# Products with the values in runs of seven key blocks, halves of one PSUM bank by turns, eight buffers of turned weights

## The chip, the cores and the metric

The kernel runs on one core of a Trainium2 chip. The metric is the device time of one launch in microseconds (us), the median of three runs; lower is better.

## The reference, cut to what matters

A transformer block in float32: `x` is 8 x 1024 x 512, 16 heads of width 32, a causal attention and a feed-forward net with blockwise four-bit rounding. Both take the same normalised input, and both results are added to `x`.

```python
xn = layernorm(x)
q, k, v = split(xn @ W_attn + b_attn)              # 16 heads of 32
att = softmax(where(causal, q @ k.T / sqrt(32), -inf))
y = (att @ v).reshape(B, S, D)                     # the products of this change
attn = y @ W_proj + b_proj
ffn = fp4_linear(silu(fp4_linear(xn, w_gate)) * fp4_linear(xn, w_up), w_down)
out = x + attn + ffn                               # fp4_linear rounds both operands, in blocks of 16
```

## The kernel before, in words

A **tile** is 128 of the 1024 rows of one batch (64 tiles), a **twin** two neighbouring tiles, a **unit** two heads of one batch (64 units). A **pair** is two neighbouring query tiles of a unit, 256 queries; a unit has pairs 0 to 3. Pair p sees 2(p+1) key blocks of 128 keys because of the causal mask, so a unit has 2 + 4 + 6 + 8 = 20 blocks.

The program has one instruction stream per engine, in the order in which the Python code emits it (`manual_schedule`); semaphores between engines are added by the framework from the tiles that each instruction reads and writes. The order is made by a planner in the kernel: six streams of work (`merge`: products with the values `weigh`, scores `scored`, the network, its quantised input, the preparation of later tiles, and `finish`) are stepped by turns. Each step states its cost on TensorE, the time from which it may start, and how many banks it needs; `clock`, `act(...)`, `dve(...)` and `pool(...)` are the planner's own reckoning of time. `Later(us, action)` emits an action when the planner's clock has passed its due time; `.now()` emits it at once.

PSUM holds six banks for everyone (`Banks`), one bank for `acc` (the network's sum) and one for `y`.

`scored` (L604 on TensorE) makes scores in a bank, VectorE finds the negated maxima (L617, L620), ScalarE writes the exponentials to one of twelve `part` buffers (L576). `weigh(un, pair)` then goes over the key blocks j of the pair: four TensorE transposes (L709) put the block's weights, keys on partitions, into a bank (two on the last, diagonal block); ScalarE copies the bank to `pr` (L712; five buffers). Blocks are gathered in `waiting`. At every fourth key block, and at the last one of the pair, the step ends with the time from which `pr` is ready, and `weighted()` emits the products of the gathered blocks without a break (L687). The blocks are taken in groups of 2; 4; 4 and 2; 4 and 4 for the four pairs, six groups or **runs** a unit. A block gives two products (one per head) with 128x32 weights, each of which is two records in the profile; even and odd blocks and the two heads go to four column positions of the array:

```python
row = (j % 2 * HU + r) * HD
nc.tensor.matmul(y[row : row + HD, base + q0 : base + QW], ...,
    start=(j < 2), stop=(j >= last - 1), tile_position=(0, row))
```

Pair 0 and 2 write columns 0 to 255 of `y`, pair 1 and 3 columns 256 to 511 (`base`). After pair 1 and after pair 3 ScalarE copies the whole bank to `yu` (L733), and two DMAs store it to `y_kept` (L739). `emptied[0]` is the planned end of that copy; the next products wait for it in the plan.

Around it: `residual` (L790) loads the rows of `x` that the network's sum of a tile is added to (`res`, two buffers; bias on GpSimd, L793), for the first tile of a twin in the middle of its sum and for the second one before the last piece of the first. `summed` (L801) adds and later stores `part_kept` (L804). `added` makes the sum (L776), eleven products for a tile. `fetch` loads what `finish` needs: two `yT`, sixteen rows of inverses, and `part` (L890, two buffers); `finish` makes the projection (L918), adds it to `part` (L923) and stores the result (L931).

`project` (L449, then ScalarE L461) makes the queries and keys: eight products of 256 columns fill the two halves of a bank, then two ScalarE instructions read a half each:

```python
for j in range(2):
    for c in range(NC):
        nc.tensor.matmul(pq[:, j, :], lhsT=halves[j][:, c, :], rhs=xnT[:, c, :], ...)
...
for j in range(2):
    nc.scalar.activation(full[:, j, :], pq[:, j, :], AF.Identity, ...)
```

Of the kernel before, what the change touches and what calls it, by code (L numbers as in the profile page):

```python
# [9 lines left out]
F32 = mybir.dt.float32  # L10
# [9 lines left out]
P = 128  # L20
# [7 lines left out]
def kernel(  # L28
# [31 lines left out]
    nc = tc.nc  # L60

    B, S, D = x.shape
# [16 lines left out]
    SOONER = 0.45  # L79
    PARTS = 12  # L80
    QUEUE = 1.0
    LATE = 0.6
    SURE = 0.4
    FILL = 0.4
# [10 lines left out]
    p2 = ctx.enter_context(tc.tile_pool(name="p2", bufs=2))  # L95
    p3 = ctx.enter_context(tc.tile_pool(name="p3", bufs=3))
    p4 = ctx.enter_context(tc.tile_pool(name="p4", bufs=4))
    p5 = ctx.enter_context(tc.tile_pool(name="p5", bufs=5))
    p8 = ctx.enter_context(tc.tile_pool(name="p8", bufs=8))
    dram = ctx.enter_context(tc.tile_pool(name="dram", bufs=6, space=DRAM))  # L100
    ps_g = ctx.enter_context(tc.tile_pool(name="ps_g", bufs=1, space=PSUM))
# [33 lines left out]
    def act(columns, after=0.0, function="other"):  # L135
        if function == "other":
            function = table[0]
        switch = TABLE if function != table[0] else 0.0
        table[0] = function
        return on("act", 0.17 + 0.00083 * columns + switch, after)  # L140
# [525 lines left out]

    def weigh(un, pair):
        f, r0 = un.u * HU // HPC, un.u * HU % HPC
        Q, first, base = pair * QT // QG, pair * QT, pair * QT % QG * P
        last = first + QT - 1  # L670
        if pair == 0:
            units_begun[0] = un.n
            if un.n + 1 < N:
                Later(1.0, lambda: load_values(units[un.n + 1]))
        while un.there.get(last) is None:
            yield 0.0, clock[0] + 0.5, 0
        if base == 0:
            un.y = ps_a.tile([P, W], F32, name="y")
        y = un.y
        waiting = []  # L680

        def weighted():
            for j, pr, q0 in waiting:
                h, jj = j // QG, j % QG
                for r in range(HU):
                    row = (j % 2 * HU + r) * HD
                    nc.tensor.matmul(  # L687
                        y[row : row + HD, base + q0 : base + QW],
                        lhsT=un.vs[h][:, jj, r * HD : (r + 1) * HD],
                        rhs=pr[:, r, q0:],  # L690
                        start=(j < 2),
                        stop=(j >= last - 1),
                        skip_group_check=True,
                        tile_position=(0, row),
                    )
            return 0.2 + 0.22 * len(waiting)

        ready = 0.0
        for j in range(last + 1):
            h = j // QG  # L700
            i0 = max(0, j - first)
            yield 0.0, un.there[last], 1
            bank, turned = banks.take()
            turned = turned.rearrange("p (r t) -> p r t", r=HU)
            for r in range(HU):
                for i in range(i0, QT):
                    part, at = un.held[first + i, h, r]
                    at += j % QG * P
                    nc.tensor.transpose(turned[:, r, i * P : (i + 1) * P], parts[part][:, at : at + P], ident)  # L709
            cost = 0.11 * HU * (QT - i0)  # L710
            pr = p5.tile([P, HU, QW], F32, name="pr")
            nc.scalar.copy(pr[:, :, i0 * P :], turned[:, :, i0 * P :])  # L712
            ready = act(HU * (QW - i0 * P), clock[0] + cost)
            banks.back(bank, ready)
            q0 = i0 * P
            if j == 1 and q0 > 0:
                nc.gpsimd.memset(pr[:, :, :q0], 0.0)
                ready = max(ready, pool(0.2))
                q0 = 0
            waiting.append((j, pr, q0))  # L720
            if j == last or j % QG == QG - 1:
                for i in range(QT):
                    for part in sorted({un.held[first + i, h, r][0] for r in range(HU)}):
                        parts_free.append(part)
                yield cost, max(ready, emptied[0]), 0
                yield weighted(), 0.0, 1
                waiting = []
            else:
                yield cost, 0.0, 1
        if last % QG < QG - 1:  # L730
            return
        yu = p2.tile([P, W], F32, name="yu")
        nc.scalar.copy(yu, y)  # L733
        emptied[0] = act(W, clock[0] + 0.3)

        def store():
            rows = slice(r0 * HD, (r0 + HU) * HD)
            for part in range(2):
                nc.sync.dma_start(  # L739
                    out=un.batch.y[part, f, rows, Q * W : (Q + 1) * W],  # L740
                    in_=yu[part * HU * HD : (part + 1) * HU * HD, :],
                )
            un.batch.units_done += Q

        Later(emptied[0] - clock[0] + 0.5, store)
        yield 0.0, 0.0, 1

    emptied = [0.0]

    def network(twins):  # L750
        emptied = [0.0]

        def down(job):
            twin = job.twin
            yield from job.hq.wait()
            twin.pieces.append((job, job.hq.done().rearrange("p (j t) -> p j t", t=QW)))
            if job.first == 0:
                twin.acc = ps_a.tile([P, D], F32, name="acc")
            if job.last:
                residual(twin.tiles[1])  # L760
            yield 0.0, max(job.hq.end, emptied[0] if job.first == 0 else 0.0), 0
            yield from added(twin, 0, *twin.pieces[-1])

# [6 lines left out]
        def added(twin, i, job, hqT):  # L770
            tl = twin.tiles[i]
            for j in range(job.count):
                n = job.first + j
                if n == NI // 2 and i == 0:
                    residual(tl)
                nc.tensor.matmul(  # L776
                    twin.acc,
                    lhsT=hqT[:, j, i * P : (i + 1) * P],
                    rhs=wdT[:, n, :],
                    start=(n == 0),  # L780
                    stop=(n == NI - 1),
                )
                if n == NI - 1:
                    summed(tl, twin.acc, clock[0] + 0.86)
                if j % 2 == 1 or j == job.count - 1:
                    yield 0.86 * (j % 2 + 1), 0.0, 0

        def residual(tl):
            tl.xr = p2.tile([P, D], F32, name="res")
            nc.sync.dma_start(out=tl.xr, in_=x[tl.b, tl.t * P : (tl.t + 1) * P, :])  # L790

            def with_bias():
                nc.gpsimd.tensor_tensor(tl.xr, tl.xr, bp, ALU.add)  # L793
                pool(1.35)

            tl.biased = Later(6.0, with_bias)

        def summed(tl, acc, after):
            xr = tl.xr
            tl.biased.now()  # L800
            nc.vector.tensor_tensor(xr, acc, xr, ALU.add)  # L801
            emptied[0] = dve(0.7, after)
            tl.part = dram.tile([P, D], F32, name="part_kept", bufs=NT + 10)
            tl.stored = Later(emptied[0] - clock[0] + 1.0, lambda: nc.sync.dma_start(out=tl.part, in_=xr))  # L804

        def product(job, wT):
            while job.twin.xqT is None:
# [60 lines left out]
    def fetch(tl):  # L868

        t = tl.t  # L870
        cols = slice(t * P, (t + 1) * P)
        if tl.b == B - 1:
            both = p3.tile([P, 2, NC, P], F32, name="ks")
            parts = [both[:, part] for part in range(2)]
            more = p3.tile([P, 2, NC, P], F32, name="qs")
            inv, part = more[:, 0], more[:, 1].rearrange("p c t -> p (c t)")
        else:
            parts = [p1.tile([P, NC, P], F32, name=f"yT{part}") for part in range(2)]
            inv = p1.tile([P, NC, P], F32, name="inv_y")
            part = p2.tile([P, D], F32, name="part")  # L880
        for k, yT in enumerate(parts):
            nc.sync.dma_start(out=yT, in_=tl.batch.y[k, :, :, cols].rearrange("f p t -> p f t"))
        heads = tl.batch.inverses.rearrange("(f u) q r t -> q u r f t", u=HPC // HU)
        for r in range(HPC):
            nc.sync.dma_start(
                out=inv[r * HD : (r + 1) * HD],
                in_=heads[t // QG, r // HU, r % HU, :, t % QG * P : (t % QG + 1) * P].partition_broadcast(HD),
            )
        tl.stored.now()
        nc.sync.dma_start(out=part, in_=tl.part)  # L890
        tl.inputs = parts[0], parts[1], inv, part
        tl.fetched = clock[0] + 6.0
# [70 lines left out]
    class Unit:  # L963
        def __init__(self, n):
            self.n, self.b, self.u = n, n // NU, n % NU
            self.qs, self.ks, self.vs, self.held, self.there = [], [], [], {}, {}

        @property
        def batch(self):
# [214 lines left out]
```

## Time and profile before

| | |
|---|---|
| time, median of 3 runs | 4106.52 us (4104.47 to 4106.9) |
| the profiled execution: its own time | 4106.01 us |
| its span, first to last instruction | 4104.2 us |
| TensorE busy, share of the span | 4007.1 us, 98% |
| VectorE, ScalarE, GpSimd busy | 3074.7 (75%), 2155.6 (53%), 150.9 us (4%) |
| mean granted TensorE clock | 0.993 |

Each row of the profile's groups names line, engine, operation, output and inputs, shapes and count, then the busy time in us, the mean duration in ns, and the idle time of the engine just before, with what ended most of it. Matmuls are pipelined: one lasts longer in the profile than the distance from its start to the next one's start, and their ends are modelled. So the cost of a product is read from the distance of starts, not from its duration.

### The profile page before, as it was taken

Reading aid. Unit: us, or ns where it says so; the run is one execution under the profiler, and the core shown is the slowest. Engines: PE = TensorE matmul, PEld = TensorE weight load, DVE = VectorE, ACT = ScalarE, POOL = GpSimd, SP = SyncE. Lnnn points to the kernel's source line nnn. Section 1 sums busy time; section 2 is a strip of 40 time slices with the busy share of each in tenths; the row PEclk is TensorE's granted clock in tenths of the full one; section 3 lists DMA queues with packets and bytes.
Section 4 is the critical chain, followed back from the end, with each engine's and each line's share of the span. In section 5 each row is a group of like instructions: output and inputs, shape, how many; then the busy total and the mean of one; then the engine's idle time right before and its main releaser. Section 6 shows DMA issues by size and latency. Waiting matters only on the chain.

```text
span 4104.2 us, 66108 instructions
## 1 busy us (share of the span) xinstructions
PE 4007.1 (98%) x22868; PEld 2998.3 (73%) x22868; DVE 3074.7 (75%) x7128; ACT 2155.6 (53%) x5342; POOL 150.9 (4%) x202
## 2 busy tenths in 40 slices
PE   8889999999999999999999999999999999999997
PEld 7767777777777777777777777777777677767675
DVE  7886777767777777777777777777767878888774
ACT  2246565555555555555555555555555555555540
POOL 0000000000000000000000000000000000000000
PEclk9989999999999999999999999999999999999999
DMA  6654444454655555555554555555554433333314
GB/s 192 197 173 132 123 123 117 135 153 141 169 155 153 156 154 143 167 156 154 154 156 144 164 156 156 152 156 146 162 152 121 116 96 91 92 92 98 96 57 128
DMA packets 550894, 572.21 MB, mean 139 GB/s; under 512 B 112416, under 2 KB 415520, under 8 KB 550560
## 3 DMA queue, kind: packets, MB, share of 16 engines
q1 hardware_dynamic: 550560, 567.99, 49.7%
q8 instruction: 181, 2.97, 0.3%
q14 instruction: 153, 1.25, 0.1%
HBM read 399.51 MB, written 168.30 MB: 138 GB/s over the span
## 4 chain that ended last, share of the span: by engine, by line
PE 92%; DVE 5%; DMA 1%; ACT 1%; issue 1%; SPq 0%; DVEq 0%; ACTq 0%
PE bank L815 29%; PE acc L776 15%; PE bank L709 11%; PE bank L449 10%; PE bank L604 8%; PE y L687 8%; PE bank L918 5%; PE bank L494 5%; PE bank L329 1%; DVE bank L620 1%; DVE hid L322 0%; DVE hid L321 0%; DVE scale L301 0%; DVE hid L320 0%; DMA qs<-inv_kept 0%
## 5 line engine op out<-in xcount | busy, mean ns | idle before, releaser
L712 ACT COPY pr<-bank 128x512 f32<-128x512 f32 (+1 forms) x1280 | 657.4, 549 | 750.3 <-PE bank L709 697.9
L576 ACT ACTIVATE part<-bank,neg 128x512 f32<-128x512 f32 (+3 forms) x1536 | 881.9, 586 | 238.6 <-DVE neg L620 228.3
L604 PE MATMUL bank<-ks,qs 128*128 128x512 f32 (+3 forms) x1536 | 701.3, 482 | 10.0 <-ACT part L576 5.4
L776 PE MATMUL acc<-wdT,hid 128*128 128x512 f32 x1408 | 672.7, 598 | 11.7 <-DVE hid L264 10.0
L815 PE MATMUL bank<-xqT,wgT 128*128 128x256 f32 x2816 | 666.9, 381 | 0.0
L709 PEld LDWEIGHTS bank<-ident,part 128*128 128x128 f32 x4608 | 548.2, 141 | 157.9 <-issue 88.7
L815 PE MATMUL bank<-xqT,wuT 128*128 128x256 f32 x2816 | 660.7, 381 | 0.1
L709 PE MATMUL bank<-ident,part 128*128 128x128 f32 x4608 | 650.4, 274 | 3.6 <-ACT part L576 3.4
L815 PEld LDWEIGHTS bank<-xqT,wuT 128*128 128x128 f32 x2816 | 520.1, 190 | 78.9 <-issue 9.4
L815 PEld LDWEIGHTS bank<-xqT,wgT 128*128 128x128 f32 x2816 | 518.0, 190 | 77.9 <-issue 16.7
L617 DVE TENSOR_REDUCE neg<-bank 128x1 f32<-128x512 f32 x512 | 351.6, 687 | 173.3 <-PE bank L604 169.1
L604 PEld LDWEIGHTS bank<-ks,qs 128*128 128x128 f32 x1536 | 280.1, 190 | 212.4 <-issue 149.9
L776 PEld LDWEIGHTS acc<-wdT,hid 128*128 128x128 f32 x1408 | 250.2, 191 | 185.4 <-issue 162.7
L620 DVE CUSTOM_DVE_ANT_0 bank<-bank,mask 128x128 f32<-128x128 f32 (+3 forms) x512 | 246.7, 507 | 152.4 <-PE bank L604 135.1
L687 PE MATMUL y<-pr,vs 128*32 128x256 f32 (+1 forms) x5120 | 356.2, 372 | 4.1 <-ACT pr L712 4.1
L620 DVE CUSTOM_DVE_ANT_0 bank<-bank,mask,neg 128x128 f32<-128x128 f32 (+3 forms) x512 | 284.5, 556 | 98.3 <-PE bank L604 81.6
L449 PE MATMUL bank<-xnT,wa 128*128 128x256 f32 x1536 | 349.7, 381 | 0.8 <-ACT part L576 0.8
L449 PEld LDWEIGHTS bank<-xnT,wa 128*128 128x128 f32 x1536 | 286.3, 190 | 48.1 <-issue 11.0
L576 ACT ACTIVATION_READ_ACCUMULATOR part<-bank,neg 128x1 f32 x1536 | 318.2, 207 | 0.0
L461 ACT ACTIVATE full<-bank,bqk 128x256 f32<-128x256 f32 x256 | 107.5, 471 | 385.7 <-PE bank L449 335.6
L832 DVE TENSOR_TENSOR hid<-hid,bank 128x512 f32<-128x512 f32 x192 | 123.6, 644 | 237.6 <-PE bank L815 237.3
L687 PEld LDWEIGHTS y<-pr,vs 128*32 128x32 f32 x5120 | 128.7, 109 | 185.1 <-issue 83.7
(79 smaller groups left out, 4255.6 us busy)
## 6 DMA issues: line engine op xcount, KB each, us to landing
wa<-in_L_attn_W_attn_dram SPq DMA_DIRECT2D x146, 512.0 KB, 3.9
qs<-qk_kept SPq DMA_DIRECT2D x512, 128.0 KB, 3.9
ks<-qk_kept SPq DMA_DIRECT2D x512, 128.0 KB, 3.8
wp<-in_L_attn_W_proj_dram SPq DMA_DIRECT2D x81, 512.0 KB, 3.6
qk_kept<-high SPq DMA_DIRECT2D x128, 256.0 KB, 3.0
qk_kept<-full SPq DMA_DIRECT2D x128, 256.0 KB, 2.9
y_kept<-yu SPq DMA_DIRECT2D x256, 128.0 KB, 2.4
yT<-y_kept SPq DMA_DIRECT2D x112, 256.0 KB, 3.9
```

The lines of the kernel that those rows point to most:

```text
L449: nc.tensor.matmul(pq[:, j, :], lhsT=halves[j][:, c, :], rhs=xnT[:, c, :], start=(c == 0), stop=(c == NC - 1),)
L494: nc.tensor.matmul(pv[:, i, :], lhsT=xnT[:, c, i * P : (i + 1) * P], rhs=wa[:, c, :], start=(c == 0), stop=(c == NC - 1),)
L576: nc.scalar.activation(parts[part][:, j * n : (j + 1) * n], banks.tiles[bank][:, j * n : (j + 1) * n], AF.Exp, bias=least, scale=1.0 if h ...
L604: nc.tensor.matmul(sc[:, j * n : (j + 1) * n], lhsT=un.qs[Q][:, r, i * P : (i + 1) * P], rhs=un.ks[h][:, r, :n], start=True, stop=True,)
L617: nc.vector.tensor_reduce(neg[:, 1, k : k + 1], one, AX.X, ALU.max, negate=True)
L620: nc.vector.tensor_tensor_reduce(one, one, mask[:, W - n :], scale=-1.0, scalar=neg[:, 1, k : k + 1] if Q else 3e38, op0=ALU.add, op1=ALU.min,
L687: nc.tensor.matmul(y[row : row + HD, base + q0 : base + QW], lhsT=un.vs[h][:, jj, r * HD : (r + 1) * HD], rhs=pr[:, r, q0:], start=(j < 2) ...
L709: nc.tensor.transpose(turned[:, r, i * P : (i + 1) * P], parts[part][:, at : at + P], ident)
L712: nc.scalar.copy(pr[:, :, i0 * P :], turned[:, :, i0 * P :])
L776: nc.tensor.matmul(twin.acc, lhsT=hqT[:, j, i * P : (i + 1) * P], rhs=wdT[:, n, :], start=(n == 0), stop=(n == NI - 1),)
L815: nc.tensor.matmul(job.g[:, j * QW : (j + 1) * QW], lhsT=wT[:, c, n * P : (n + 1) * P], rhs=job.twin.xqT[:, c, :], start=(c == 0), stop=(c ...
L918: nc.tensor.matmul(po, lhsT=yT[:, c, :], rhs=wp[:, c, :], start=(c == 0), stop=(c == NC - 1))
```

## The change

`weigh` gathers blocks in `un.waiting`, across the borders of pairs, and emits products when seven blocks wait or the unit's last block is reached: runs of 7, 7 and 6 blocks, three a unit. The `y` tile is taken once for the whole kernel; pair p uses its half p % 2. As soon as the last block of a pair has been emitted, inside the run, `empty` emits ScalarE's copy of that half (128x256) to `yu`, now four copies a unit, and plans two DMAs of 64 KB each. `pr` has eight buffers. To make room, `res` and `part` have one buffer instead of two and `yu` is half as wide; the load of `res` for a twin's second tile comes 4 us after the first tile's sum, and `fetch` first emits the store of the tile before.

```diff
+    RUN = 7
-    p5 = ctx.enter_context(tc.tile_pool(name="p5", bufs=5))
...
-        if base == 0:
-            un.y = ps_a.tile([P, W], F32, name="y")
-        y = un.y
-        waiting = []
         def weighted():
-            for j, pr, q0 in waiting:
+            cost = 0.2 + 0.22 * len(un.waiting)
+            for j, pr, q0, pair in un.waiting:
                 h, jj = j // QG, j % QG
+                base, last = pair % 2 * QW, pair * QT + QT - 1
                 for r in range(HU):
                     ...
-            return 0.2 + 0.22 * len(waiting)
+                if j == last:
+                    emptied[pair % 2] = clock[0] + cost
+                    empty(pair)
+            un.waiting = []
+            return cost
+
+        def empty(pair):
+            yu = p2.tile([P, QW], F32, name="yu")
+            base = pair % 2 * QW
+            nc.scalar.copy(yu, y[:, base : base + QW])
+            emptied[pair % 2] = act(QW, emptied[pair % 2])
+
+            def store():
                ...
+                un.batch.units_done += pair == PAIRS - 1
+            Later(emptied[pair % 2] - clock[0] + 0.5, store)
...
-            pr = p5.tile([P, HU, QW], F32, name="pr")
+            pr = p8.tile([P, HU, QW], F32, name="pr")
...
-            waiting.append((j, pr, q0))
+            un.waiting.append((j, pr, q0, pair))
             if j == last or j % QG == QG - 1:
                ...
-                yield cost, max(ready, emptied[0]), 0
+            if len(un.waiting) == RUN or j == NT - 1:
+                yield cost, max(ready, emptied[pair % 2]), 0
                 yield weighted(), 0.0, 1
...
+    emptied = [0.0, 0.0]
+    y = ps_a.tile([P, W], F32, name="y")
...
-            if job.last:
-                residual(twin.tiles[1])
...
                 if n == NI - 1:
-                    summed(tl, twin.acc, clock[0] + 0.86)
+                    if i > 0:
+                        twin.second.now()
+                    summed(tl, twin.acc, clock[0] + 0.86, twin if i == 0 else None)
...
-            tl.xr = p2.tile([P, D], F32, name="res")
+            tl.xr = p1.tile([P, D], F32, name="res")
...
+            if twin is not None:
+                twin.second = Later(emptied[0] - clock[0] + 4.0, lambda: residual(twin.tiles[1]))
...
+        if tl.n > 0 and tl.b < B - 1 and tiles[tl.n - 1].written is not None:
+            tiles[tl.n - 1].written.now()
...
-            part = p2.tile([P, D], F32, name="part")
+            part = p1.tile([P, D], F32, name="part")
```

More of the change, by code (lines that the diff above doesn't have):

```diff
@@ L668, in weigh @@
         f, r0 = un.u * HU // HPC, un.u * HU % HPC
-        Q, first, base = pair * QT // QG, pair * QT, pair * QT % QG * P
+        first = pair * QT
         last = first + QT - 1
@@ L695, in weighted @@
                     )
-            return 0.2 + 0.22 * len(waiting)
+                if j == last:
[9 more added lines that the diff above has]
+            def store():
+                rows = slice(r0 * HD, (r0 + HU) * HD)
+                for part in range(2):
+                    nc.sync.dma_start(
+                        out=un.batch.y[part, f, rows, pair * QW : (pair + 1) * QW],
+                        in_=yu[part * HU * HD : (part + 1) * HU * HD, :],
+                    )
+                un.batch.units_done += pair == PAIRS - 1
+            Later(emptied[pair % 2] - clock[0] + 0.5, store)
         ready = 0.0
@@ L724, in weigh @@
                         parts_free.append(part)
-                yield cost, max(ready, emptied[0]), 0
+            if len(un.waiting) == RUN or j == NT - 1:
+                yield cost, max(ready, emptied[pair % 2]), 0
                 yield weighted(), 0.0, 1
-                waiting = []
             else:
                 yield cost, 0.0, 1
[L730 to L748, printed above, removed]
+    emptied = [0.0, 0.0]
+    y = ps_a.tile([P, W], F32, name="y")
     def network(twins):
@@ L796, in residual, with summed @@
             tl.biased = Later(6.0, with_bias)
-        def summed(tl, acc, after):
+        def summed(tl, acc, after, twin):
             xr = tl.xr
@@ L965, in __init__ @@
             self.n, self.b, self.u = n, n // NU, n % NU
-            self.qs, self.ks, self.vs, self.held, self.there = [], [], [], {}, {}
+            self.qs, self.ks, self.vs, self.waiting, self.held, self.there = [], [], [], [], {}, {}
         @property
```

## The prediction

> **What bounds the kernel now.** I read the page first, then TensorE's waits, then the tile view of `y`, the groups by form, and the timeline around single runs. From the page:
>
> ```profile
> PE 4007.1 (98%) x22868; PEld 2998.3 (73%) x22868; DVE 3074.7 (75%) x7128; ACT 2155.6 (53%) x5342; POOL 150.9 (4%) x202
> L687 PE MATMUL y<-pr,vs 128*32 128x256 f32 (+1 forms) x5120 | 356.2, 372 | 4.1 <-ACT pr L712 4.1
> ```
>
> TensorE is busy for 98%, and the two largest entries among its waits are small:
>
> ```profile
> PE bank L329 <- DVE hid L322: 20.7, 7, 4.6
> PE bank L329 <- DVE xt L383: 15.9, 1, 15.9
> ...
> PE y L687 <- ACT pr L712: 4.1, 8, 0.5
> ```
>
> So nothing else is to be won by waiting less: time is saved only by taking less of TensorE, and every new idle time of TensorE adds to the end in full. In the windows of 1000 to 2000 and 2000 to 3000 us TensorE is busy for 1000.00 of 1000.
>
> What a run costs beside its products is read from starts on the timeline of TensorE:
>
> ```profile
> 2004.36 3.62 PE L494 MATMUL bank<-wa,xnT 128*128 128x256 f32 x16
> 2007.91 0.63 PE L687 MATMUL y<-pr,vs 128*32 128x256 f32 x8
> 2008.47 1.99 PE L918 MATMUL bank<-wp,yT 128*128 128x256 f32 x8
> ...
> 2048.05 1.06 PE L687 MATMUL y<-pr,vs 128*32 128x256 f32 x16
> 2049.03 0.44 PE L604 MATMUL bank<-ks,qs 128*128 128x384 f32 x1
> ```
>
> Records of 256 columns follow each other by 0.216 us (L494: median of 961 distances). In a run four records, one per column position, start within 0.02 us, and the next four 0.216 us later (0.240 after the first four). So 8 records (two blocks) need 0.432 us and 16 need 0.864; from the run's start to the next work the trace has 0.568 and 1.003 us in the mean of 128 and 256 runs. That is 0.14 us too much at the way out. On the way in, the record before a run stands 0.309 us ahead of it where it is a 256-column one of L815 (99 runs, 0.093 us too much); after a score product of L604 (196 runs) it is 0.508 against 0.333 ahead of other work (0.175). The mean over the 384 runs is 0.13. One run less saves 0.27 us.
>
> **The change part by part.**
>
> *Half as many runs.* 6 become 3 a unit, 192 fewer: 192 x 0.27 = -52 us. Bounds: 192 x 0.14 = -26 (if the way in costs the same elsewhere) and 192 x 0.31 = -60.
>
> *Runs of odd length.* Even and odd blocks use different column positions, so a stretch takes as long as its longer side. Before, stretches of 2, 4, 4, 2, 4, 4 blocks gave 10 x 0.432 = 4.32 us a unit. Now the unit is cut at the runs and at the ends of pairs into 2 | 4 | 1, 5 | 2, 6 blocks: 0.432 + 0.864 + 0.432 + 1.08 (three odd blocks, the last of half width) + 0.432 + 1.296 = 4.54. 64 x 0.216 = +14 us.
>
> *Copies inside the run.* This is the part that decides. `empty` puts ScalarE's copy of one half of `y` between products, and the products behind it write the other half of the same bank. Whether they wait for the copy is shown by a case of the same shape, L449 and L461, where ScalarE's first instruction reads half of a bank and the second the other half:
>
> ```profile
> 2037.46 3.62 PE L449 MATMUL bank<-xnT,wa 128*128 128x256 f32 x16
> ...
> 2041.12 0.84 ACT L461 ACTIVATE full<-bank,bqk 128x256 f32<-128x256 f32 x2 [4.85 <-PE bank L449]
> ```
>
> The first half is complete after 8 of the 16 records, near 2037.46 + 7 x 0.216 + 0.38 = 2039.4, and ScalarE has been idle for 4.85 us; yet it starts at 2041.12, 0.04 after the last record of the other half. A bank is guarded as a whole. In the other direction, which counts here, the kernel before has six places where a TensorE write to columns 128 to 255 of a bank waits for exactly the ScalarE instruction that reads columns 0 to 127 of it; in the other 204 places of disjoint columns a wait that was already passed covers it. So TensorE waits at every copy that is followed by products in its run: after pair 0 and pair 1 in the first run, after pair 2 in the second. After pair 3 the run ends, and the next one is far off. 3 x 64 = 192 waits, one for each switch that is saved.
>
> The Trainium skill speaks against this part: PSUM — Partial Sum Buffer, section "PSUM bank collisions raise a hardware error", has the rule "Semaphore-guard PSUM by bank × quadrant (by bank is the simple version), not by address", since two engines on one bank and the same 32 partitions collide even at different columns. By that rule the 192 waits stand and the sum is the +126 us below; guarded by address it would be the -23 of the third case. No run here shows a collision.
>
> The price of one wait, ScalarE being free, from the tile view of `y` (durations as least, median and most; then what ScalarE waited for ahead of its copy, us and times) and the groups by form:
>
> ```profile
> L687 PE MATMUL y<-pr,vs x5120: 272/379/637, 253.1 to 3978.7; 128*32 128x256 f32 x167, 128*32 128x128 f32 x30
> ...
>   PE y L687: 155.0, 92
> ```
>
> ```profile
> L712 ACT COPY pr<-bank 128x256 f32<-128x256 f32 x256 | 96.9, 379 | 26.7 <-PE bank L709 26.7
> L733 ACT COPY yu<-y 128x512 f32<-128x512 f32 x128 | 75.1, 587 | 155.1 <-PE y L687 155.0
> ```
>
> From the start of the last product: 0.379 to its end; 0.080 from there to the copy's start (each of the 92 copies that waited for TensorE, out of 128); 0.379 for a copy of 128x256; 0.052 from a ScalarE end to TensorE's start (the 8 waits of L687 for L712); 0.024 more in the first four records; less the 0.216 that the next start would have taken anyway. That is 0.698 us, and 192 x 0.698 = +134 us. Nothing lies beside it: TensorE works in order, and behind the waiting product stand the rest of the run and all other streams.
>
> ScalarE is not always free. In this run the copy that belongs to the products at 2048.05 (over at 2049.11) starts 2.46 us late, since an exponential ahead of it waits for VectorE:
>
> ```profile
> 2050.33 0.69 ACT L576 ACTIVATE part<-bank,neg 128x512 f32<-128x512 f32 x1 [2.29 <-DVE neg L620]
> ...
> 2051.57 0.58 ACT L733 COPY yu<-y 128x512 f32<-128x512 f32 x1
> ```
>
> Before, that cost nothing, since the products that need the bank were planned later. Taking for all 384 runs what the code emits to ScalarE ahead of the run's products, and when it ended in the trace: in 126 runs it ends later than a copy could start, in the mean over all 0.43 us after a whole run and 0.53 after its first two blocks. Per unit two waits meet such a queue (the second one of the first run finds it drained). Bounds: 0, and 64 x (0.43 + 0.53) = +61. I take half, +30: TensorE is some 1.5 us later per run than the planner reckons, time in which ScalarE and VectorE catch up.
>
> *What is covered.* 256 copies of 0.379 instead of 128 of 0.587: +22 us on ScalarE, which is idle for 1949. 256 more DMA issues on SP, about 0.4 us each, 100 us of a queue that spends most of its time waiting; behind them stand the loads of keys, queries and weights, for which TensorE waited less than 5 us in all. Eight buffers of `pr` are what a run of seven needs. `res`: the load at 4 us after the first sum has behind it 3.3 us to landing and 1.3 for the bias, 8.6 in all, against the 11 x 0.86 = 9.5 us of the second sum; if that cover is gone, 32 twins x about 1 us. `part`: the store goes out ahead of some 18 issues of `fetch`, longer than the 4.9 us it takes to land. I cost all of this at nothing.
>
> *Sum*, against the profiled execution's 4106.0 us (0.5 below the median of the three): -52 + 14 + 134 + 30 = +126, **4232 us**, slower by 3.1%.
>
> **The rivals.**
>
> *ScalarE late at every first copy.* Same waits, but the queue ahead of the copy holds exponentials that wait for VectorE nearly each time: a late queue costs 0.434 x 384 / 126 = 1.32 us, and at 128 copies 169 us in place of 30: 4371. It decides from about two late copies in three. For it: runs of seven come when scores are dense. Against it: one in three is late now.
>
> *A single `res` or `part` in the way.* SP waits for a buffer, and loads behind it come late. At a whole landing of 2.4 us for each of 64 tiles, 64 x 2.4 = +154 on top: 4386. Against it: TensorE waits for DMA nowhere now.
>
> *Halves that are independent* (the faster side). If products wait only for a copy of their own half, one dependency in a run is left: pair 2's first block on pair 0's copy, with pair 1's 0.864 us between, more than the 0.62 that a free ScalarE takes, so only its late cases count, some 15 us. -52 + 14 + 15 = -23, 4083. It decides as soon as TensorE's row for L687 shows no wait for L733. Against it: the six waits on disjoint columns, and L461.
>
> **How the numbers follow.** 0.82 for the forecast, 0.09 for the late ScalarE, 0.03 for the single buffers, 0.06 for independent halves. The forecast's own bounds are -60 + 14 + 134 + 0 = +88 (4194) and -26 + 14 + 134 + 61 = +183 (4289). The range is reached a little below for the planner's new order of all streams, and up toward the late ScalarE: 4175 to 4325. About 0.2% (8 us) is what a measurement can tell from no change. Faster has the independent halves, 0.06; within 0.2% 0.01; slower 0.93.
>
> **What would show it.** Right: TensorE's waits get a new first entry, `y` L687 for `yu` L733, 100 to 200 us over up to 192 waits; 192 runs, of which 128 are broken by idle times; distances at ways in and out as before. The idle share of TensorE rises from 2% to about 5%. Wrong: no such entry (then the third case), or that entry far over 200 us (the first rival), or waits for DMA or for `res` L801 beside it (the second).

## The result and the profile after

The changed kernel takes 4270.42 us (median of 4 runs, 4265.94 to 4275.31), the kernel before 4105.5 us on the same chip (4 runs, 4102.65 to 4106.9). The ratio is 1.0398 (95% interval 1.0385 to 1.0411): slower by 4.0%, 165 us; 4232 us were forecast, with 4175 to 4325 as the range. The profiled execution took 4265.94 us with a span of 4264.2 us, 160 us longer than before. First the page of the changed kernel: busy times and shares of the span, and the group of the products with the values.

```profile
PE 4017.3 (94%) x22868; PEld 3042.2 (71%) x22868; DVE 3087.4 (72%) x7128; ACT 2173.7 (51%) x5470; POOL 147.1 (3%) x202
...
L685 PE MATMUL y<-pr,vs 128*32 128x256 f32 (+1 forms) x5120 | 371.0, 373 | 100.3 <-ACT yu L703 100.3
```

The same 22868 records on TensorE (PE), but 247 us of its span are idle instead of 97. TensorE's waits (in total, times, longest) have a new first entry:

```profile
PE y L685 <- ACT yu L703: 100.3, 192, 0.8
...
PE bank L820 <- DVE xqT L264: 21.7, 8, 2.7
PE bank L604 <- ACT part L576: 19.3, 35, 2.5
...
PE bank L820 <- ACT pr L731: 13.1, 18, 0.7
PE bank L728 <- ACT pr L731: 7.2, 20, 0.4
```

192 times, three a unit, products of `y` wait for the copy of `y`; the longest wait is 0.8 us. The other four rows are waits that had little or no weight before (0, 5.4, 0 and 0.2 us). One run on the timeline, TensorE and then ScalarE (start, duration, count, and in brackets the idle time ahead of it):

```profile
2002.66 0.64 PE L685 MATMUL y<-pr,vs 128*32 128x256 f32 x8
2003.79 1.06 PE L685 MATMUL y<-pr,vs 128*32 128x256 f32 x16 [0.49 <-ACT yu L703]
2005.40 0.62 PE L685 MATMUL y<-pr,vs 128*32 128x256 f32 x4 [0.55 <-ACT yu L703]
2005.95 0.45 PE L604 MATMUL bank<-ks,qs 128*128 128x384 f32 x1
```

```profile
2003.37 0.37 ACT L703 COPY yu<-y 128x256 f32<-128x256 f32 x1
2004.97 0.37 ACT L703 COPY yu<-y 128x256 f32<-128x256 f32 x1 [1.23 <-PE y L685]
```

Read it across: 8 records (pair 0) end at 2003.30, the copy runs from 2003.37 to 2003.74, the next 16 (pair 1, the other half of the bank) start at 2003.79; they end at 2004.85, the copy follows from 2004.97 to 2005.34, and the last block (4 records) starts at 2005.40. A run of seven blocks takes 3.29 us here.

The whole span by kind of record, each record counted from its start to the start of the next one, less waits over 0.02 us. Waits inside a run or right behind it stand in the first row, waits right ahead of a run in the second (4.1 us before, for `pr`; none after); all others are in the third:

| us | before | after | difference | in the forecast |
|---|---|---|---|---|
| runs, from start to the next work (384; 192) | 329.4 | 458.0 | +128.5 | -26 + 14 + 134 + 30 |
| records just ahead of a run, and all scores | 582.8 | 555.1 | -27.7 | -26 |
| all other waits | 73.6 | 127.3 | +53.7 | 0 |
| everything else | 3098.5 | 3104.3 | +5.8 | 0 |
| together | | | +160 | +126 |

### The profile page after: what moved, and what is told of

It reads as the page before. It is cut to its first block, busy times and chain, and to the rows that moved or that the text cites. A ratio compares the mean times of both kernels' runs of the same rounds, so it can differ in the third digit from the quotient of the medians.

```text
span 4264.2 us, 66564 instructions
## 1 busy us (share of the span) xinstructions
PE 4017.3 (94%) x22868; PEld 3042.2 (71%) x22868; DVE 3087.4 (72%) x7128; ACT 2173.7 (51%) x5470; POOL 147.1 (3%) x202
## 5 line engine op out<-in xcount | busy, mean ns | idle before, releaser
L604 PE MATMUL bank<-ks,qs 128*128 128x512 f32 (+3 forms) x1536 | 729.9, 497 | 22.7 <-ACT part L576 19.3
L820 PE MATMUL bank<-xqT,wgT 128*128 128x256 f32 x2816 | 673.8, 384 | 35.5 <-DVE xqT L264 21.7
L728 PE MATMUL bank<-ident,part 128*128 128x128 f32 x4608 | 661.3, 275 | 12.2 <-ACT pr L731 7.2
L685 PE MATMUL y<-pr,vs 128*32 128x256 f32 (+1 forms) x5120 | 371.0, 373 | 100.3 <-ACT yu L703 100.3
L685 PEld LDWEIGHTS y<-pr,vs 128*32 128x32 f32 x5120 | 142.0, 109 | 293.9 <-ACT yu L703 179.3
```

Source lines behind the costliest of these rows:

```text
L604: nc.tensor.matmul(sc[:, j * n : (j + 1) * n], lhsT=un.qs[Q][:, r, i * P : (i + 1) * P], rhs=un.ks[h][:, r, :n], start=True, stop=True,)
L685: nc.tensor.matmul(y[row : row + HD, base + q0 : base + QW], lhsT=un.vs[h][:, jj, r * HD : (r + 1) * HD], rhs=pr[:, r, q0:], start=(j < 2) ...
L820: nc.tensor.matmul(job.g[:, j * QW : (j + 1) * QW], lhsT=wT[:, c, n * P : (n + 1) * P], rhs=job.twin.xqT[:, c, :], start=(c == 0), stop=(c ...
```

## The experiments

Two theories stood against each other. **Guarded bank:** the copy of one half and the products into the other half use one bank and wait for each other. **Order:** runs of seven in a row leave ScalarE and VectorE without work, and the waits for the copy are only where that shows.

### A bank for each half of `y`, and its partner with one bank less

PSUM has eight banks, all in use, so two banks for `y` leave five for everyone. The partner has five as well and keeps `y` in one bank: it has the first line of the edit, and not those marked "two banks only".

```diff
-            self.tiles = [ps_g.tile([P, W], F32, name=f"bank{k}") for k in range(6)]
+            self.tiles = [ps_g.tile([P, W], F32, name=f"bank{k}") for k in range(5)]
...
-                        y[row : row + HD, base + q0 : base + QW],
+                        y[pair % 2][row : row + HD, q0:],                 # two banks only
...
-    y = ps_a.tile([P, W], F32, name="y")
+    y = [ps_a.tile([P, QW], F32, name=f"y{half}") for half in range(2)]   # two banks only
```

The partner:

> The changed kernel with five banks for everyone instead of six, one bank of PSUM left unused: the partner of the run with two banks for y, which needs that bank. Theory of the guarded bank (TensorE waits at 192 copies inside runs, 0.51 us of idle time each, since products and copy use one bank): all 192 waits stay, about 98 us of idle time before L685 for the copy; the time is that of the changed kernel plus what one bank less costs, 0 to 60 us, 4270 to 4330. Theory of the order (runs of seven in a row leave ScalarE and VectorE without work and late afterwards, the waits for the copy being only where that shows): the same range.

The two banks:

> As the five-bank partner, in the same order of instructions, but each half of y has a bank of its own. Guarded bank: products no longer wait for the copy of the other half; one dependency is left (pair 2's first block on pair 0's copy, 0.86 us of products between). The 100 us of waits for yu go, TensorE wins 192 x 0.70 = 134 us or a little more against the partner (ScalarE is blocked for less time as well): 120 to 160 us less. Theory of the order: the idle time turns up at other instructions, less than 40 us gained.

Measured: 4364.0 us for the partner (ratio to the kernel before 1.0635, 1.0619 to 1.0651), over its range; 4220.12 us with two banks (1.0278, 1.0263 to 1.0294), 144 us less, inside the range. A sixth bank for everyone is worth some 94 us (4364.0 against 4270.4). The first row of TensorE's waits in the partner, and what is left of it with two banks:

```profile
PE y L685 <- ACT yu L703: 121.3, 192, 1.9
```

```profile
PE y L685 <- ACT yu L702: 12.9, 26, 1.0
```

The runs take 475.4 us in the partner and 332.9 with two banks, 142 us of the 144. All other waits are 157.7 and 158.6 us, so taking the copies' waits away moves no waiting elsewhere. That is the guarded bank. The 26 waits that remain are the one true dependency that the prediction named, of pair 2's first block on pair 0's copy.

### The copies behind the run

Runs of 6, 8 and 6 blocks, and the copies emitted when the run's products are out. No pair begins in a half that is still to be copied.

```diff
+    RUN_ENDS = ((1, 3), (3, 1), (3, 7))      # pair, key block
...
                 if j == last:
-                    emptied[pair % 2] = clock[0] + cost
-                    empty(pair)
+                    full.append(pair)
+            for pair in full:
+                emptied[pair % 2] = clock[0] + cost
+                empty(pair)
...
-            if len(un.waiting) == RUN or j == NT - 1:
-                yield cost, max(ready, emptied[pair % 2]), 0
+            if (pair, j) in RUN_ENDS:
+                yield cost, max(ready, *emptied), 0
```

> The changed kernel with runs of 6, 8 and 6 blocks, that end with pair 1, with pair 3's second block and with the unit, and the copies of y emitted behind a run's last product: still three runs a unit, one bank for y, all 20 blocks in even groups, no product behind a copy in its run. Guarded bank: no wait for yu is left; against the kernel before 192 x 0.27 = 52 us are saved, nothing is added but what the new order costs (0 to 30 us): 4055 to 4085, faster than both. Theory of the order: long runs themselves cost, 4110 or more.

Measured: 4062.09 us (4 runs, 4058.39 to 4062.88), ratio 0.9894 (0.9879 to 0.9908), inside the range. It beats both kernels, the changed one by 208 us with as many runs. On its page and among its groups:

```profile
PE 3954.6 (97%) x22868; PEld 3048.0 (75%) x22868; DVE 3064.9 (75%) x7128; ACT 2162.0 (53%) x5470; POOL 147.8 (4%) x202
...
L686 PE MATMUL y<-pr,vs 128*32 128x256 f32 (+1 forms) x5120 | 320.5, 373 | 0.0
```

No idle time is left ahead of a product with the values, against 100.3 us in the changed kernel. Of the 52 us that the fewer runs were to save, 44 arrive: -22 in the runs, -31 in the records ahead of them and the scores (4 of them the waits for `pr`), +12 in other waits, -3 in the rest.

### The same order, with the copies inside the runs

The kernel of 6, 8 and 6 blocks, but `empty` stands where the change has it. On all five engines the instructions are in the same order as in the kernel above.

> The kernel with runs of 6, 8 and 6 blocks once more, but each copy of a half of y is emitted behind its pair's last block, inside the run. On every engine the instructions stand in the same order as in its partner with the copies behind the runs; only the waits differ: TensorE waits behind pair 0 and behind pair 2, 128 times. Guarded bank: 128 x 0.70 = 89 us over the partner's 4062, 4140 to 4160, and TensorE's other waits stay at the partner's 86 us. If a wait inside a run also makes ScalarE and VectorE late for what comes later, the other waits grow as in the changed kernel (by 50 us) and the time is over 4180.

Measured: 4180.68 us (ratio 1.018, 1.0165 to 1.0195), 119 us more than its partner; 89 were expected. The guarded bank's second claim, that the other waits stay, holds, and its price is too low. The time lies just inside the range of the second theory (over 4180), but the growth of the other waits, on which that theory rests, is absent. By kind of record, only the runs differ: 307.0 us in the partner, 425.1 here, +118.1; every other kind stays within 3 us, and all other waits are 85.8 and 84.3 us.

```profile
PE y L685 <- ACT yu L703: 92.1, 128, 1.7
PE bank L329 <- DVE hid L322: 21.9, 7, 4.6
```

128 waits of the bare 0.511 us of idle time (0.080 + 0.379 + 0.052) would be 65.4; the 92.1 hold 26.7 us in which ScalarE was still at something else when the products were done. Without these, a wait costs (118.1 - 26.7) / 128 = 0.714 us, against 0.698 in the prediction.

### Runs of six

```diff
-    RUN = 7
+    RUN = 6
```

> The changed kernel with RUN = 6: runs of 6, 6, 6 and 2 blocks, four a unit, of which only the first has a copy inside (behind pair 0). Guarded bank: 128 fewer switches, -35 us; 64 waits, +45 us; all groups even, +0: 4116 and what the order costs, 4105 to 4150. Theory that runs that go across pairs cost by themselves: about as slow as the changed kernel, 4200 or more.

Measured: 4114.36 us (ratio 1.0019, 1.0009 to 1.0029). Runs of 6, 6, 6 and 2, and one wait a unit (64 in all, 35.2 us): what the saved switches bring and what the waits cost cancel. This fits a cost that goes with the copies inside the runs, but it doesn't set that apart from a cost of runs that cross pairs, since only the first run of a unit still crosses a border, with the one copy in it. The two kernels of one order do: their runs of 6, 8 and 6 cross pairs with and without copies inside.

### The buffers alone

```diff
-    p5 = ctx.enter_context(tc.tile_pool(name="p5", bufs=5))
+    p5 = ctx.enter_context(tc.tile_pool(name="p5", bufs=7))
...
-            tl.xr = p2.tile([P, D], F32, name="res")
+            tl.xr = p1.tile([P, D], F32, name="res")
...
-            part = p2.tile([P, D], F32, name="part")
+            part = p1.tile([P, D], F32, name="part")
```

With them go the later load of `res` and the earlier store in `fetch`, as in the change.

> The kernel before with its six runs a unit and its whole copies of y, and only the rest of the change: one buffer for res and for part instead of two, the load of the second tile's rows 4 us after the first sum, the store of the tile before ahead of fetch, and seven buffers of turned weights (eight do not fit beside the wide yu). My sum costs this at nothing: 4095 to 4115. If the 64 us that the changed kernel lost beyond my sum without a late ScalarE (4106 + 96) come from here, 4150 to 4175.

Measured: 4106.36 us, ratio 1.0 (0.999 to 1.001). Single buffers, moved loads and more `pr` cost and bring nothing while the runs are as before.

### A planner that knows of the waits

```diff
-            cost = 0.2 + 0.22 * len(un.waiting)
+            cost = 0.2 + 0.22 * len(un.waiting) + 0.7 * sum(j == 2 * p + 1 for j, _, _, p in un.waiting[:-1])
```

> The changed kernel, but its planner reckons 0.7 us more for every copy inside a run, so that its clock is right about these waits. If the 54 us of ordinary waits that the changed kernel has more than the kernel before come from a planner that does not know of the waits, they shrink to 90 us or less in all, and the time is 4220 to 4245. If they belong to the order that runs of seven give, or to chance in the order, they stay between 100 and 150 us, and the time is 4255 to 4285. The 100 us of waits for yu stay in both.

Measured: 4242.33 us (ratio 1.0331, 1.0316 to 1.0347), 28 us less than the changed kernel. The waits for the copies stay (101.2 us, 192 times); all other waits fall from 127.3 to 104.1 us, not to 90. So the time lies in the first theory's range and the waits between the two. A right clock gives a better order, but not the one without extra waits, and it doesn't tell a wrong clock from luck in the order: this run changes both.

### Runs of 6, 7 and 7 blocks

The copies stay behind the runs; one block moves from the second run to the third.

```diff
-    RUN_ENDS = ((1, 3), (3, 1), (3, 7))
+    RUN_ENDS = ((1, 3), (3, 0), (3, 7))
```

> Runs of 6, 7 and 7 blocks with the copies behind the runs: no wait for a copy, three runs a unit, but the second and third run have an odd number of blocks. If a stretch takes as long as its longer side, 64 x 0.216 = 14 us over the runs of 6, 8 and 6, 4070 to 4085 (a run of 6, 8, 6 uses all eight buffers, a run of seven leaves one: if that is worth anything it is less). If odd numbers cost nothing, 4055 to 4065.

Measured: 4198.05 us (ratio 1.0224, 1.0209 to 1.0239), far outside both ranges, from moving one block. The odd numbers are not the reason. A unit's three runs have medians of 1.419, 1.851 and 1.637 us, against 1.419, 1.851 and 1.419 with 6, 8 and 6: +0.218 us, 14 us in all, as reckoned. The rest is a new wait in the order that the planner made of it, with a second effect behind it (timeline of TensorE; then the table of windows: length, busy time and count of each engine, granted TensorE clock, DMA share, GB/s):

```profile
1564.94 1.89 PE L823 MATMUL bank<-xqT,wuT 128*128 128x256 f32 x8
1572.42 0.79 PE L604 MATMUL bank<-ks,qs 128*128 128x512 f32 x1 [5.58 <-DVE hid L840]
1573.14 3.20 PE L686 MATMUL y<-pr,vs 128*32 128x256 f32 x28
```

```profile
1564.00:1570.80 6.80, 2.84 (x17) 2.24 (x15) 0.69 (x1) 0.86 (x2) 0.00 (x0) 1.00 0.90 279
1570.80:1577.60 6.80, 5.18 (x35) 2.98 (x36) 5.85 (x16) 1.21 (x5) 1.65 (x3) 0.50 0.01 4
1577.60:1584.00 6.40, 6.40 (x32) 5.23 (x30) 4.36 (x11) 2.11 (x8) 0.00 (x0) 1.00 0.38 102
```

```profile
PE bank L604 <- DVE hid L840: 77.5, 17, 5.6
```

17 times a score product waits some 4.6 us for a bank that VectorE's product of the gate and the other half of the network has yet to give back, and the granted clock is at 0.50 afterwards: the run of 28 records shown takes over 3.0 us to the next work instead of 1.637. Against 6, 8 and 6 the span is 134 us longer: other waits +75, runs +42 (14 of them the odd numbers, most of the rest the half clock), records ahead of runs and scores +16. In the first window TensorE and VectorE do little while DMA moves 279 GB/s. What VectorE waits for there is a load, that of `xt` (rows of `x` for the preparation of later tiles); its waits for this load are, first with 6, 7 and 7 and then with 6, 8 and 6:

```profile
DVE stats L376 <- DMA xt<-in_L_attn_x_dram: 145.8, 19, 9.4
```

```profile
DVE stats L376 <- DMA xt<-in_L_attn_x_dram: 5.5, 3, 3.2
```

Each of the 17 waits of TensorE has one of these ahead of it, of 6.3 to 9.4 us. In the case shown VectorE waits 9.39 us, until 1570.08; the product of the gate and the other half (L840), which gives back the bank, stands behind that in VectorE's stream and starts at 1571.69, and TensorE goes on at 1572.42. So the late load is the first cause; why this order has it late stays open.

## Why the prediction was right, and where it was off

**The deciding step held.** Copies inside the runs make TensorE wait 3 x 64 = 192 times because the bank is guarded as a whole. The count is 192 in the trace, and the two-bank pair and the pair with one order show that these waits are the loss: 144 us for 192 waits and 119 us for 128. The rule of the Trainium skill (PSUM — Partial Sum Buffer, section "PSUM bank collisions raise a hardware error") on guarding by bank and not by address agrees with that; a collision itself is in no run here. One thing the runs don't separate: here every bank is one tile of the program, and two banks for `y` are two tiles. The waits are semaphores that the framework adds, and whether it guards by bank or by tile, and what the chip does without them, is not shown.

**Its size held.** 0.698 us were reckoned for one wait. The pair with one order gives 0.714 without late ScalarE. In the changed kernel the runs grew by 128.5 us, against -26 + 14 + 134 = 122 without the late ScalarE.

**The saving held.** -52 us were split into 26 at the ways out of the runs and 26 at the ways in. Records ahead of runs and scores together fell by 27.7 us, 4.1 of them the waits for `pr`. With 6, 8 and 6, where nothing is added, 44 us came in the time. One reading behind it is wrong: 0.508 against 0.333 for a score ahead of a run compares scores that themselves stand behind different records. Behind the same record (a product of 256 columns of the network) it is 0.508 against 0.421, and behind one of 512 columns 0.727 against 0.634. So the way in costs 0.09 us, the same as behind L815, and a run 0.23, which makes -44 of the -52. That the time fell by just that is partly chance, since the other waits rose by 12 with 6, 8 and 6. The price of odd runs, 0.216 us a unit, was 0.218.

**Late ScalarE was mis-sized for this order.** +30 were taken from bounds of 0 and 61. The 192 waits hold 100.3 us, and 192 x 0.511 is 98.1: 2 us. With 6, 8 and 6 and the copies inside it is 27 us, in the five-bank partner 23. So it depends on the order, and reading it off the order before gave a bound and not a value. The reason for taking half, that TensorE is some 1.5 us later per run, does not follow from the prediction's own sum: 134 us over 192 runs are 0.7 us.

**The step that failed is the order, costed at nothing.** All other waits grew by 53.7 us: 21.7 where the network's products wait for the quantised input (8 times, all late in the span), 13.1 where they wait for a bank that ScalarE's copy to `pr` holds, and some 21 of growth in the waits of scores and transposes for ScalarE. The buffers alone cost nothing, and TensorE's wait for `res` is 1.7 us in both kernels, so they don't come from `res` and `part` by themselves; the two pairs show that waits for a copy don't make other waits longer; a planner that knows of the waits loses 23 us less. What remains is that six streams were put in another order; this is argued by what is left and not shown. Which of the planner's choices makes these waits stays open. That the profiled execution lies 34 us over the forecast is mostly this term (+54), less the late ScalarE that did not come (-28): two misses of opposite sign, and that they offset each other is luck.

**The rivals.** Independent halves are excluded. ScalarE late at every first copy did not happen: 3 of the 192 waits are over 0.6 us. Single buffers in the way: excluded with the old runs, not tried with the new ones. (Their price was taken at 2.4 us a landing, where the load of `res` takes 3.3.)

## What to carry to other kernels

An accumulator that is emptied in halves still is one bank: here a copy of 128x256 between two groups of products cost TensorE 0.7 us, its own 0.38 us and both ways of the signal, even though the columns are different. Put the copy behind the whole run, and choose the runs' ends so that none begins in a half that is still full; as few runs then gained 1.1% instead of losing 4.0%. In a kernel whose order comes from a planner, any change of a step re-orders everything: one block moved from one run to the next cost 136 us, so measure several neighbours before judging an idea.

## What the runs showed that was not expected

The granted clock was 0.50 in single pieces or several in a row of 3.41 us, with records of 256 columns 0.427 us apart instead of 0.216. The pieces inside the span add up to 61 us before and 99 us in the changed kernel. Many follow a long wait of TensorE: there is one behind each of the 17 waits of 2.4 to 5.6 us with 6, 7 and 7, but behind only four of the eight waits of 2.71 us for the quantised input in the changed kernel, and one in the kernel before (from 3228.0 us) has only waits of 0.42, 0.24 and 0.17 us just ahead. So no limit for a single wait follows from these traces. Some of the changed kernel's +5.8 us of other records may be this clock; no run separates it. The Trainium skill (TensorE: Matmul & The Clock Gate, section "HAM oscillation — how this bites in real kernels") describes a return to half rate after an idle window of some 3.4 us. The pieces of 3.413 us agree with that length, but here waits of 2.71 us were enough four times.

A score product's distance to the next record depends on what stands ahead of it: in the kernel before, at the full clock and with other work than a run behind, 512 columns take 0.234 us behind another score (mostly one of 384 columns), 0.335 behind a run, 0.421 behind a product of 256 columns of the network and 0.634 behind one of 512. So a saved way into a run can return in part as a costlier score elsewhere, and only the two together can be compared.
